# Triangle update: one stage for norm and fill, left and right through DRAM by eighths, products with strided operands

## The chip, the cores and the metric

The kernel runs on one core of a Trainium2 chip. The metric is the device time of one execution in microseconds (us), lower is better. The median of three runs before the change is 5121.33 us.

## The reference

An image of 256 x 256 positions with 128 channels (float32) passes through four layers, each of which normalises its input, applies an operation and adds the result to the input. The layers are a triangle attention, a gated recurrence, a triangle multiplication and a 3 x 3 convolution. The change touches only the third, whose core is:

```python
x = x + _L2_conv_ref(_gn(x), ...)          # layer 3 of 4; _gn normalises groups of 4 channels

pair_norm = layer_norm(pair, ln_in_w, ln_in_b)                       # over the 128 channels
p = jnp.einsum('bijd,hd->bijh', pair_norm, p_in_w)                   # 256 outputs: left 128, right 128
g = jax.nn.sigmoid(jnp.einsum('bijd,hd->bijh', pair_norm, g_in_w))
left = g[..., :H] * p[..., :H]
right = g[..., H:] * p[..., H:]
out = jnp.einsum('bikd,bjkd->bijd', left, right / jnp.float32(L))    # a 256 x 256 x 256 product per channel
out = layer_norm(out, ln_out_w, ln_out_b)
out = jnp.einsum('bijh,dh->bijd', out, p_out_w)
gate = jax.nn.sigmoid(jnp.einsum('bijd,ed->bije', pair_norm, g_out_w))
return gate * out
```

## The kernel before

Images lie in DRAM with the channel as the partition: `x2T` (the layer's input), `znT` (the normalised input), `prodD` (the products), `x3T` (the output), each 128 x 65,536 float32, 33.5 MB. The method `triangle` works on them in three stages, one after the other on the same core. Every operation in it is pinned, so each engine runs its operations in the order in which the program states them; `mm`, `act`, `tt`, `add` and `table` are such pinned forms of a matmul, a ScalarE activation, a VectorE product, a VectorE addition and a ScalarE table load. A float32 matmul in the source appears in the trace as two matmul instructions, each with its own weight load.

**Stage one (norm).** 32 loads of 2048 positions each. `load` brings `xin` from `x2T` on SyncE's queue. `centre` multiplies 1024 positions by a centring matrix (`zc`, a PSUM tile) and adds a bias (`zs`); `square` squares it on ScalarE; `variance` takes the mean over channels with four small matmuls (`var`) and forms `rs` = (var + eps)^-0.5 by `Ln` and `Exp`; `spreads` brings `rs` back to all partitions (`pr`). VectorE multiplies `zs` by `pr` to `zn`, GpSimd applies the affine part, and GpSimd's queue stores `zn` to `znT`. The activation tables of Ln and Exp and of the sigmoid are different ones, and each switch is a table load on ScalarE.

**Stage two (fill and products).** Four quarters of 32 channels. In each, all of `znT` is read again (`zt`, 64 blocks of 1024 positions); a chunk of 128 positions is the stationary operand and 128 columns of `wf` (32 channels for left and right, gate and value) are the moving one:

```python
for ch in range(8):
    o = (b % 2) * 1024 + ch * P
    mm(z[:, ch, :], zt[:, o:o + P], wf[:, g].rearrange("c t d -> c (t d)"))
```

ScalarE takes the sigmoid of the gates (`sg`), and VectorE writes value times gate into `LR`, which keeps a whole quarter in SBUF with the row index innermost, so that its elements are written 512 bytes apart. Then 32 products follow, one for each channel, each of four source matmuls with contiguous operands of `LR` into a PSUM tile `po`; ScalarE scales them into `o`, and GpSimd's queue stores `o` (256 KB) to `prodD`.

**Stage three** reads `znT`, `prodD` and `x2T` and makes `x3T`. Ahead of it `transformed_taps` prepares the convolution's weights. Neither is changed.

Of the kernel before, what the change touches and what calls it, by code (L numbers as in the profile page):

```python
# [9 lines left out]
F32 = mybir.dt.float32  # L10
# [7 lines left out]
P = 128  # L18
# [12 lines left out]
class Kernel:  # L31
# [24 lines left out]
    def table(self, name, key="table"):  # L56
        return self.chain(key, self.nc.scalar.preload_act_table_set(name))

    def mm(self, out, lhsT, rhs, start=True, stop=True):
        return self.nc.tensor.matmul(out, lhsT, rhs, start=start, stop=stop)  # L60
# [985 lines left out]
                        D[it - lag]["b"] = it - lag  # L1046
                        step(D[it - lag])

    def triangle(self, x2T, x3T, znT, prodD, stats2, shift2, stats3, prepare):

        nc, tc, I = self.nc, self.tc, self.i
        V = nc.vector
        NB, G, CQ = NPIX // 1024, 4, P // 4
        pin = lambda f: lambda *a, **k: tc.keep_in_program_order(f(*a, **k))  # L1056
        mm, act, copy = pin(self.mm), pin(self.act), pin(nc.scalar.copy)
        tt, ts, stt, bn = pin(V.tensor_tensor), pin(V.tensor_scalar), pin(V.scalar_tensor_tensor), pin(V.bn_stats)
# [3 lines left out]
        with ExitStack() as c:  # L1062
            wp = c.enter_context(self.pool(name="tw", bufs=1))
            with self.pool(name="twp", bufs=2, space=PSUM) as ps0:
                ab = self.group_affine(wp, ps0, stats2, self.g4, "2", shift=shift2)
                lc, cb = self.centering(wp, ps0, ab, "2")
                W = self.weights
                lnw, lnb, low, lob = (W[n] for n in ("in_w", "in_b", "out_w", "out_b"))
                wpg, oraw, we = W, W["o"], W["e"]
                pb = ps0.tile([P, 2], F32, name="tpbo", tag="gn")  # L1070
                self.mm(pb[:, 0:1], oraw, lob)
                wbo = wp.tile([P, 1], F32, name="twbo")
                V.tensor_copy(wbo, pb[:, 0:1])
                wo = wp.tile([P, P], F32, name="two")
                V.tensor_scalar_mul(wo, oraw, low)

                wf = wp.tile([P, G, 4, CQ], F32, name="wf")
                for n, m in enumerate("gp"):
                    for side in range(2):
                        V.tensor_copy(wf[:, :, 2 * n + side, :],  # L1080
                                      wpg[m][:, side * P:(side + 1) * P].rearrange("c (g d) -> c g d", g=G))

            quarters = c.enter_context(ExitStack())
            zp = quarters.enter_context(self.pool(name="tz", bufs=5))

# [7 lines left out]
            def variance(ps, work, sq):  # L1093

                var = ps.tile([P, 512], F32, name="var", tag="r", bufs=2)
                for k in range(4):
                    mm(var[32 * k:32 * k + 32], m32, sq[k // 2][:, (k % 2) * 512:(k % 2 + 1) * 512])
                rs = work.tile([P, 512], F32, name="rs")
                act(rs, var, AF.Ln, bias=self.eps)
                act(rs, rs, AF.Exp, scale=-0.5)  # L1100
                return rs

            def spreads(ps, rs):
                pr = [ps.tile([P, 1024], F32, name="pr", tag="w") for _ in range(2)]
                for k in range(4):
                    mm(pr[k // 2][:, (k % 2) * 512:(k % 2 + 1) * 512], spread[32 * k:32 * k + 32], rs[32 * k:32 * k + 32])
                return pr


            with ExitStack() as c1:  # L1110
# [3 lines left out]
                xin, sq, zs = {}, {}, {}  # L1114

                def load(m):
                    if m < NB // 2:
# [3 lines left out]
                def centre(m, b):  # L1121
                    if m >= NB // 2:
                        return
                    zc = ps.tile([P, 1024], F32, name="zc", tag="w")
                    for k in range(2):
                        s = b * 1024 + k * 512
                        mm(zc[:, k * 512:(k + 1) * 512], lc, xin[m][:, s:s + 512])
                    zs[m, b] = work.tile([P, 1024], F32, name="zs")
                    add(zs[m, b], zc, cb)

                def square(m, b):
                    if m < NB // 2:
# [3 lines left out]
                table(LN_EXP)  # L1136
                for m in range(2):
                    load(m)
                for b in range(2):
                    centre(0, b)  # L1140
                    square(0, b)
                for m in range(NB // 2):
                    load(m + 2)
                    centre(m + 1, 0)
                    rs = variance(ps, work, [sq[m, b] for b in range(2)])
                    square(m + 1, 0)
                    centre(m + 1, 1)
                    square(m + 1, 1)
                    pr = spreads(ps, rs)
                    zn = io.tile([P, 2048], F32, name="zn")  # L1150
                    for b in range(2):
                        z = zn[:, b * 1024:(b + 1) * 1024]
                        tt(z, zs[m, b], pr[b], MUL)
                        nc.gpsimd.tensor_scalar(z, z, lnw, lnb, MUL, ADD)
                    nc.gpsimd.dma_start(znT[:, m * 2048:(m + 1) * 2048], zn)

            with ExitStack() as c1:

                LR = c1.enter_context(self.pool(name="tl", bufs=1)).tile([P, 2, 2, 2 * CQ, P], F32, name="LR")
                work = c1.enter_context(self.pool(name="t2w", bufs=2))  # L1160
                io = c1.enter_context(self.pool(name="t2", bufs=3))
                ps = c1.enter_context(self.pool(name="t2s", bufs=2, space=PSUM))
                table(SIGMOID)
# [27 lines left out]
            quarters.close()  # L1191
            prepare(W["kt"], W["wd"], W["bv"])


# [270 lines left out]
    def run(self, ctx):  # L1465
# [12 lines left out]
        biasD = dram.tile([NH, NPIX], F32, name="biasD")  # L1478
        HD_ = dram.tile([2, 2 * KS, 4, N, HC // 4], F32, name="HD")
        prodD = image("prodD")  # L1480
        self.early = {n: [const.tile([P, 2], F32, name=f"early{k}{n}") for k in range(2)] for n in "3"}
        later = ctx.enter_context(self.pool(name="lw", bufs=1))
        with self.pool(name="aw", bufs=1) as wp:
# [10 lines left out]
        self.triangle(x2T, x3T, znT, prodD, stats["2"], shift2, stats["3"], lambda *a: self.transformed_taps(late(), *a))  # L1494
        self.convolution(x3T, stats["3"], late())


# [56 lines left out]
```

## Time and profile before

| | us |
|---|---|
| median of three runs | 5121.33 (5119.53 to 5126.31) |
| profiled execution, its own time | 5126.96 |
| profiled execution, span from the first to the last instruction | 5125.2 |
| mean granted TensorE clock | 0.988 of full speed |
| triangle, stage one: first `zc` to first `z` | 3243.6 to 3457.2 |
| triangle, stage two: first `z` to last `po` | 3457.2 to 4146.9 |
| triangle, stage three | from 4159.2 |

The durations come from the profiled execution, and its span is 1.8 us shorter than its own time. Times of the triangle are counted from the start of the span. In the profile, PE is TensorE's matmul, PEld its weight load, DVE is VectorE, ACT is ScalarE, POOL is GpSimd and SP is SyncE. A row of a group names the line, the engine, the operation, the written tile, the read tiles and their shapes, and how often it occurs, and then the busy time of the group (overlaps counted once), the mean duration of one in ns, and the time the engine stood idle ahead of it, with what ended that. L60 is the line of the helper through which every matmul goes, L54 that of every activation, L1056 that of the pinned operations of `triangle`, so these groups are told apart by their tiles.

### The profile page before, as it was taken

The page shows a single profiled execution, that of the slowest core. Times are in us where ns is not written, and L with a number is a line of the kernel's source. Part 1 is how long each engine was busy: PE and PEld are TensorE (multiplying, and loading weights), DVE is VectorE, ACT ScalarE, POOL GpSimd, SP SyncE. Part 2 cuts the span into 40 slices and gives each one's busy share as a digit, 9 for nine tenths or more (in the row PEclk, how much of TensorE's full clock was granted, in tenths as well). Part 3 has the DMA queues.
Part 4 walks back from the last instruction along what each step waited for, and adds up shares of the span by engine and source line. Part 5 has one row for each costly group of instructions (what it writes and reads, how often), then busy time and mean ns, then how long its engine had stood idle before and what let it go on. Part 6 is the DMA issues. An engine that isn't in the chain of part 4 may idle for free.

```text
span 5125.2 us, 78589 instructions
## 1 busy us (share of the span) xinstructions
PE 4948.5 (97%) x31357; PEld 2702.7 (53%) x31357; DVE 4100.7 (80%) x4797; ACT 3496.2 (68%) x4948; POOL 414.2 (8%) x600
## 2 busy tenths in 40 slices
PE   7999999999999899999999999899999989989999
PEld 2444555555555333333333333229999953349999
DVE  6666999999999799999999999675333537779886
ACT  5445888888888799999999999453333357762110
POOL 1332000000000000000000000240111010000000
PEclk9999999999999899999999999999999999999999
DMA  8794222222222122222222222687666678865432
GB/s 282 277 338 186 83 79 87 83 80 87 83 80 82 59 76 63 76 63 76 63 76 63 76 63 67 253 304 280 239 229 238 237 277 325 327 224 188 140 121 67
DMA packets 205054, 781.44 MB, mean 152 GB/s; under 512 B 56857, under 2 KB 60263, under 8 KB 155423
## 3 DMA queue, kind: packets, MB, share of 16 engines
q1 hardware_dynamic: 147070, 505.57, 29.3%
q0 software_dynamic: 56320, 270.42, 14.5%
q8 instruction: 250, 4.10, 0.3%
q14 instruction: 118, 0.96, 0.1%
q10 hardware_dynamic: 1296, 0.40, 0.0%
HBM read 504.94 MB, written 271.32 MB: 151 GB/s over the span
## 4 chain that ended last, share of the span: by engine, by line
PE 56%; DVE 28%; issue 5%; ACT 1%; DMA 1%; POOL 0%; POOLq 0%; DVEq 0%; SPq 0%; ACTq 0%
PE z L60 9%; PE m L60 7%; PE nd L60 7%; PE sc L60 5%; PE po L60 4%; PE zc L60 4%; DVE tr L896 3%; DVE t L893 3%; DVE y L893 3%; DVE p L893 3%; DVE yf L893 3%; PE ppq L60 3%; PE ppv L60 2%; PE px L60 2%; PE pe L60 2%
## 5 line engine op out<-in xcount | busy, mean ns | idle before, releaser
L559 DVE TENSOR_TENSOR e<-sc,bT 128x1024 f32<-128x1024 f32 x512 | 603.2, 1220 | 52.4 <-PE sc L60 51.2
L54 ACT ACTIVATE e<-e 128x1024 f32<-128x1024 f32 x512 | 540.5, 1056 | 63.0 <-DVE e L559 49.2
L1056 DVE TENSOR_TENSOR LR<-z,sg 128x512 f32<-128x512 f32 x256 | 268.2, 1049 | 365.0 <-ACT sg L54 365.0
L60 PE MATMUL m<-U,v 128*128 128x128 f32 x4608 | 517.6, 276 | 6.6 <-DVE v L1403 6.6
L60 PEld LDWEIGHTS m<-U,v 128*128 128x128 f32 x4608 | 517.4, 193 | 6.7 <-DVE v L1403 6.7
L60 PE MATMUL z<-wf,zt 128*128 128x128 f32 x4096 | 460.4, 276 | 2.1 <-DVE zn L1056 1.3
L60 PEld LDWEIGHTS z<-wf,zt 128*128 128x128 f32 x4096 | 460.0, 193 | 3.9 <-DVE zn L1056 2.8
L54 ACT ACTIVATE sg<-z 128x512 f32<-128x512 f32 x256 | 152.8, 597 | 309.9 <-PE z L60 308.0
L54 ACT ACTIVATE sq<-zs 128x1024 f32<-128x1024 f32 x192 | 202.4, 1054 | 196.4 <-DVE zs L370 156.8
L559 DVE TENSOR_TENSOR ks<-e 128x1024 f32<-128x1024 f32 x256 | 300.9, 1217 | 0.0
L60 PE MATMUL sc<-tq,tk 32*128 32x256 f32 x4096 | 298.2, 403 | 2.8 <-DVE e L559 1.9
L60 PE MATMUL nd<-e,tv 128*32 128x256 f32 x4096 | 272.0, 383 | 0.0
L60 PEld LDWEIGHTS sc<-tq,tk 32*128 32x128 f32 x4096 | 187.3, 185 | 160.5 <-issue 97.1
L54 ACT ACTIVATE dn<-dn 128x512 f32<-128x512 f32 x384 | 241.7, 629 | 13.3 <-DVE dn L559 2.6
L60 PE MATMUL av<-y,ident 128*128 128x512 f32 x384 | 191.3, 607 | 44.9 <-DVE y L893 44.9
L60 PE MATMUL po<-LR 128*128 128x256 f32 x1024 | 222.2, 380 | 6.9 <-DVE LR L1056 6.9
L1440 ACT COPY m4s<-m 128x512 f32<-128x512 f32 x32 | 18.7, 584 | 287.8 <-PE m L60 287.8
L60 PEld LDWEIGHTS po<-LR 128*128 128x128 f32 x1024 | 194.1, 190 | 34.2 <-DVE LR L1056 7.7
L60 PE MATMUL bx<-p,ident 128*128 128x512 f32 x384 | 193.3, 612 | 0.0
L54 ACT ACTIVATE o<-po 128x256 f32<-128x256 f32 x256 | 84.3, 381 | 145.4 <-issue 110.5
L60 PEld LDWEIGHTS nd<-e,tv 128*32 128x32 f32 x4096 | 120.3, 110 | 109.8 <-issue 44.2
L862 ACT ACT_TABLE_LOAD x132 | 169.4, 1283 | 1.6
(368 smaller groups left out, 10276.9 us busy)
## 6 DMA issues: line engine op xcount, KB each, us to landing
zt<-znT SPq DMA_DIRECT2D x128, 1024.0 KB
znT<-zn POOLq DMA_DIRECT2D x64, 1024.0 KB, 5.3
xin<-x2T SPq DMA_DIRECT2D x64, 1024.0 KB
xin<-in_x_dram SPq DMA_DIRECT2D x50, 1024.0 KB
xr<-x3T SPq DMA_DIRECT2D x46, 768.0 KB
xT<-xo POOLq DMA_DIRECT2D x32, 1024.0 KB, 9.2
xr<-xT SPq DMA_DIRECT2D x64, 512.0 KB
zn<-znT SPq DMA_DIRECT2D x64, 512.0 KB
```

The source lines that it names most:

```text
L54: return self.nc.scalar.activation(out, in_, func, bias=bias, scale=scale, **kw)
L60: return self.nc.tensor.matmul(out, lhsT, rhs, start=start, stop=stop)
L559: pin = lambda f: lambda *a, **k: tc.keep_in_program_order(f(*a, **k))
L862: pin(nc.scalar.preload_act_table_set(want))
L893: pin(V.tensor_tensor(out, a, b_, op))
L896: pin(V.scalar_tensor_tensor(out, a, k, b_, op0, op1))
L1056: pin = lambda f: lambda *a, **k: tc.keep_in_program_order(f(*a, **k))
L1440: nc.scalar.copy(m4, m[4])
```

## The change

The channels are now cut into eight eighths of 16 (`G, CQ = 8, P // 8`). Stage one and the fill become one stage: behind the norm of 2048 positions, all 256 channels of left and right are made at once from `zn` in SBUF, with 512 columns of `wf` as the moving operand. They go to a new DRAM image `LRD` of 8 x 128 x 16,384 float32, ordered by eighths. `znT` is still stored, but read only by stage three. The products then read one eighth at a time from `LRD` in four loads of 2 MB; the tile `LR` has two buffers of 64 KB per partition, and in it the channel lies innermost, so that both operands of a product matmul step over 128 elements (512 bytes) from one element to the next. The order of operations in the new stage is written out by hand, two loads at a time, with the table switched twice for each pair.

```diff
-        NB, G, CQ = NPIX // 1024, 4, P // 4
+        NB, G, CQ = NPIX // 1024, 8, P // 8
...
-                wf = wp.tile([P, G, 4, CQ], F32, name="wf")
+                wf = wp.tile([P, 2, G, 2, CQ], F32, name="wf")
...
+                            zs[m, b] = work.tile([P, 1024], F32, name="zs", bufs=8)
+                            add(zs[m, b], zc, cb)
+                        load(m + 2)
...
+                def scales(ms):
+                    var = {}
+                    for m in ms:
+                        var[m] = ps.tile([P, 512], F32, name="var", tag="r", bufs=2)
+                        for k in range(4):
+                            mm(var[m][32 * k:32 * k + 32], m32, sq[m, k // 2][:, (k % 2) * 512:(k % 2 + 1) * 512])
+                    table(LN_EXP)
+                    for m in ms:
+                        rs[m] = work.tile([P, 512], F32, name="rs")
+                        act(rs[m], var[m], AF.Ln, bias=self.eps)
+                        act(rs[m], rs[m], AF.Exp, scale=-0.5)
+                    table(SIGMOID)
+
+                def normalise(m):
+                    if m < NM:
+                        pr = spreads(ps, rs[m])
+                        zn[m] = work.tile([P, 2048], F32, name="zn")
+                        for b in range(2):
+                            z = zn[m][:, b * 1024:(b + 1) * 1024]
+                            tt(z, zs[m, b], pr[b], MUL)
+                            nc.gpsimd.tensor_scalar(z, z, lnw, lnb, MUL, ADD)
+                        nc.gpsimd.dma_start(znT[:, m * 2048:(m + 1) * 2048], zn[m])
+
+                def left_right(m, i):
+                    if not i:
+                        st[m] = work.tile([P, G, 4, 4, 2 * CQ], F32, name="st", bufs=2)
+                    z = ps.tile([P, 2, 512], F32, name="z", tag="w")
+                    for j in range(2):
+                        o = (2 * i + j) * P
+                        mm(z[:, j], zn[m][:, o:o + P], wf.rearrange("c n g s d -> c (n g s d)"))
+                    sg = work.tile([P, 2, 256], F32, name="sg")
+                    act(sg, z[:, :, :256], AF.Sigmoid)
+                    k = 2 * (i % 2)
+                    tt(st[m][:, :, i // 2, k:k + 2].rearrange("p g k f -> p k g f"),
+                       z[:, :, 256:].rearrange("p k (g f) -> p k g f", g=G), sg.rearrange("p k (g f) -> p k g f", g=G), MUL)
+                    if i == 7:
+                        nc.gpsimd.dma_start(LRD[:, :, m * 512:(m + 1) * 512].rearrange("g p n -> p g n"),
+                                            st[m].rearrange("p g x k f -> p g (x k f)"))
...
+                for m in range(0, NM, 2):
+                    for i in range(8):
+                        left_right(m, i)
+                    if m + 2 < NM:
+                        scales((m + 2, m + 3))
+                        centre(m + 4)
+                        centre(m + 5)
+                        normalise(m + 2)
+                    for i in range(8):
+                        left_right(m + 1, i)
+                        if i == 1:
+                            normalise(m + 3)
+                        if i % 2:
+                            square(m + 4 + i // 4, i // 2 % 2)
...
-                for g in range(G):
-
-                    for b in range(NB):
-                        if b % 2 == 0:
-                            zt = zp.tile([P, 2048], F32, name="zt")
-                            nc.sync.dma_start(zt, znT[:, b * 1024:(b + 2) * 1024])
-                        z = ps.tile([P, 8, P], F32, name="z", bufs=3)
-                        for ch in range(8):
-                            o = (b % 2) * 1024 + ch * P
-                            mm(z[:, ch, :], zt[:, o:o + P], wf[:, g].rearrange("c t d -> c (t d)"))
-                        sg = work.tile([P, 8, 2 * CQ], F32, name="sg")
-                        act(sg, z[:, :, :2 * CQ], AF.Sigmoid)
-                        rows = lambda t: t.rearrange("p (x q) f -> p x q f", x=2)
-                        tt(LR[:, :, :, :, 2 * b:2 * b + 2].rearrange("p a k f x -> p x (a k) f"),
-                           rows(z[:, :, 2 * CQ:]), rows(sg), MUL)
...
+                lp = c1.enter_context(self.pool(name="tl", bufs=2))
                 io = c1.enter_context(self.pool(name="t2", bufs=3))
-                ps = c1.enter_context(self.pool(name="t2s", bufs=2, space=PSUM))
+                ps = c1.enter_context(self.pool(name="t2s", bufs=4, space=PSUM))
                 for g in range(G):
+                    LR = lp.tile([P, P, 4, 2 * CQ], F32, name="LR")
+                    flat_lr = LR.rearrange("p x k f -> p (x k f)")
+                    for n in range(4):
+                        cols = slice(n * 4096, (n + 1) * 4096)
+                        nc.sync.dma_start(flat_lr[:, cols], LRD[g, :, cols])
                     for d in range(CQ):
                         po = ps.tile([P, 2, 2, P], F32, name="po")
                         for a in range(2):
                             for kc in range(2):
-                                mm(po[:, a], LR[:, a, kc, d, :], LR[:, :, kc, CQ + d, :], start=kc == 0, stop=kc == 1)
+                                mm(po[:, a], LR[:, :, 2 * a + kc, d],
+                                   LR[:, :, kc::2, CQ + d].rearrange("p x b -> p b x"), start=kc == 0, stop=kc == 1)
```

More of the change, by code (lines that the diff above doesn't have):

```diff
@@ L1047, in recurrence, with triangle @@
                         step(D[it - lag])
-    def triangle(self, x2T, x3T, znT, prodD, stats2, shift2, stats3, prepare):
+    def triangle(self, x2T, x3T, znT, prodD, LRD, stats2, shift2, stats3, prepare):
         nc, tc, I = self.nc, self.tc, self.i
         V = nc.vector
-        NB, G, CQ = NPIX // 1024, 4, P // 4
+        NB, G, CQ = NPIX // 1024, 8, P // 8
         pin = lambda f: lambda *a, **k: tc.keep_in_program_order(f(*a, **k))
@@ L1075, in triangle @@
                 V.tensor_scalar_mul(wo, oraw, low)
-                wf = wp.tile([P, G, 4, CQ], F32, name="wf")
+                wf = wp.tile([P, 2, G, 2, CQ], F32, name="wf")
                 for n, m in enumerate("gp"):
                     for side in range(2):
-                        V.tensor_copy(wf[:, :, 2 * n + side, :],
+                        V.tensor_copy(wf[:, n, :, side, :],
                                       wpg[m][:, side * P:(side + 1) * P].rearrange("c (g d) -> c g d", g=G))
-            quarters = c.enter_context(ExitStack())
-            zp = quarters.enter_context(self.pool(name="tz", bufs=5))
             m32 = wp.tile([P, 32], F32, name="tmean")
@@ L1107, in spreads @@
                 return pr
+            NM = NB // 2
             with ExitStack() as c1:
@@ L1113, in triangle, with centre @@
                 ps = c1.enter_context(self.pool(name="t1s", bufs=3, space=PSUM))
-                xin, sq, zs = {}, {}, {}
+                xin, sq, zs, rs, zn, st = {}, {}, {}, {}, {}, {}
                 def load(m):
-                    if m < NB // 2:
+                    if m < NM:
                         xin[m] = io.tile([P, 2048], F32, name="xin")
                         nc.sync.dma_start(xin[m], x2T[:, m * 2048:(m + 1) * 2048])
[L1121 to L1129, printed above, removed]
+                def centre(m):
+                    if m < NM:
+                        for b in range(2):
+                            zc = ps.tile([P, 1024], F32, name="zc", tag="w")
+                            for k in range(2):
+                                s = b * 1024 + k * 512
+                                mm(zc[:, k * 512:(k + 1) * 512], lc, xin[m][:, s:s + 512])
+                            zs[m, b] = work.tile([P, 1024], F32, name="zs", bufs=8)
+                            add(zs[m, b], zc, cb)
+                        load(m + 2)
@@ L1131, in square @@
                 def square(m, b):
-                    if m < NB // 2:
+                    if m < NM:
                         sq[m, b] = work.tile([P, 1024], F32, name="sq")
                         act(sq[m, b], zs[m, b], AF.Square)
-                table(LN_EXP)
+                def scales(ms):
[10 more added lines that the diff above has]
+                    table(SIGMOID)
@@ new lines, in normalise @@
+                def normalise(m):
+                    if m < NM:
+                        pr = spreads(ps, rs[m])
+                        zn[m] = work.tile([P, 2048], F32, name="zn")
+                        for b in range(2):
+                            z = zn[m][:, b * 1024:(b + 1) * 1024]
+                            tt(z, zs[m, b], pr[b], MUL)
+                            nc.gpsimd.tensor_scalar(z, z, lnw, lnb, MUL, ADD)
+                        nc.gpsimd.dma_start(znT[:, m * 2048:(m + 1) * 2048], zn[m])
@@ L1137, in triangle @@
                 for m in range(2):
                     load(m)
[L1139 to L1150, printed above, removed]
-                    for b in range(2):
[L1152 to L1155, printed above, removed]
+                for m in range(2):
+                    centre(m)
+                    for b in range(2):
+                        square(m, b)
@@ new lines, in triangle @@
+                scales((0, 1))
+                for m in range(2, 4):
+                    centre(m)
+                for m in range(2):
+                    normalise(m)
+                for m in range(2, 4):
+                    for b in range(2):
+                        square(m, b)
+                for m in range(0, NM, 2):
[12 more added lines that the diff above has]
+                            square(m + 4 + i // 4, i // 2 % 2)
@@ L1157, in triangle @@
             with ExitStack() as c1:
-                LR = c1.enter_context(self.pool(name="tl", bufs=1)).tile([P, 2, 2, 2 * CQ, P], F32, name="LR")
-                work = c1.enter_context(self.pool(name="t2w", bufs=2))
+                lp = c1.enter_context(self.pool(name="tl", bufs=2))
                 io = c1.enter_context(self.pool(name="t2", bufs=3))
-                ps = c1.enter_context(self.pool(name="t2s", bufs=2, space=PSUM))
-                table(SIGMOID)
+                ps = c1.enter_context(self.pool(name="t2s", bufs=4, space=PSUM))
@@ L1189, in triangle @@
                                             o.rearrange("p a j b -> p a (j b)"))
-            quarters.close()
             prepare(W["kt"], W["wd"], W["bv"])
@@ L1480, in run @@
         prodD = image("prodD")
+        LRD = dram.tile([8, P, NPIX // 4], F32, name="LRD")
         self.early = {n: [const.tile([P, 2], F32, name=f"early{k}{n}") for k in range(2)] for n in "3"}
@@ L1492, in late @@
             return pools[0]
-        self.triangle(x2T, x3T, znT, prodD, stats["2"], shift2, stats["3"], lambda *a: self.transformed_taps(late(), *a))
+        self.triangle(x2T, x3T, znT, prodD, LRD, stats["2"], shift2, stats["3"], lambda *a: self.transformed_taps(late(), *a))
         self.convolution(x3T, stats["3"], late())
```

## The prediction

> **What bounds the kernel now.** I read the page's busy shares first, then the chain of waits, then the busy time by stretches of the stages that the diff touches, then the groups with their shapes.
>
> ```profile
> PE 4948.5 (97%) x31357; PEld 2702.7 (53%) x31357; DVE 4100.7 (80%) x4797; ACT 3496.2 (68%) x4948; POOL 414.2 (8%) x600
> ```
>
> TensorE is busy almost throughout, so a change must take TensorE time away or fill its gaps. The chain (start us, length us, engine, tile, line, count) shows what the triangle's second stage is made of:
>
> ```profile
> 3632.04 114.36 PE z L60 x1024
> 3748.12 55.67 PE po L60 x256
> ...
> 4204.82 3.43 PE py L60 x8
> ```
>
> One quarter is 1024 fill matmuls in 114.36 us (111.7 ns each, 128 columns) and 256 product matmuls in 55.67 us (217 ns, 256 columns). The third row gives 512 columns: 3.43/8 = 429 ns. All three are 0.84 to 0.87 ns a column: TensorE itself is the limit. (Each float32 matmul of the source is two instructions; counts are instructions.)
>
> Stretches (us, busy of each engine, granted clock, DMA share, GB/s):
>
> ```profile
> 3300.00:3440.00 140.00, 130.00 (x520) 39.62 (x524) 103.18 (x88) 71.20 (x86) 62.67 (x64) 0.99 0.91 342
> 3305.00:3310.00 5.00, 5.00 (x21) 1.40 (x20) 1.80 (x2) 2.26 (x3) 0.57 (x1) 0.73 1.02 433
> 3465.00:3578.00 113.00, 110.73 (x983) 110.39 (x984) 66.28 (x64) 37.01 (x62) 0.00 (x0) 1.00 0.83 294
> 3578.00:3632.00 54.00, 54.00 (x253) 47.54 (x252) 0.00 (x0) 20.40 (x62) 16.73 (x31) 1.00 0.40 153
> ```
>
> The first stage (first row) repeats every 6.33 us and moves 342 GB/s, near what DMA gives; its TensorE columns need far less than its busy time suggests: 8 centring matmuls (3.43 us) and two bursts of 8 small ones (var 1.06, pr 1.14 us in the timeline, of which 0.16 each is drain) make 5.3 us. The second row is the highest DMA rate, 433 GB/s; from 3270 to 3315 us it is 391 to 433, and I use 415. Fill and products (last rows) are pure TensorE. The tile's first and last times give the whole: first zc at 3243.6, first z at 3457.2, last product at 4146.9 us: **903.3 us**, of which 213.6 before the fill.
>
> The groups that price the new operands (engine, operation, tiles, shapes, count | busy us, mean ns | idle before):
>
> ```profile
> L60 PE MATMUL po<-LR 128*128 128x256 f32 x1024 | 222.2, 380 | 6.9 <-DVE LR L1056 6.9
> L1056 DVE TENSOR_TENSOR LR<-z,sg 128x512 f32<-128x512 f32 x256 | 268.2, 1049 | 365.0 <-ACT sg L54 365.0
> L893 DVE TENSOR_TENSOR d<-pa,ff 128x512 f32<-128x512 f32 x64 | 43.2, 675 | 4.4 <-PE pa L60 4.4
> L181 ACT COPY H<-ph 128x512 f32<-128x512 f32 x16 | 16.5, 1032 | 20.5 <-PE ph L60 20.5
> L1440 ACT COPY m4s<-m 128x512 f32<-128x512 f32 x32 | 18.7, 584 | 287.8 <-PE m L60 287.8
> ```
>
> Rows two and four write 512 elements to SBUF with steps of 512 and 64 bytes, rows three and five write them contiguously: 1049 against 675 ns, 1032 against 584. A step costs 0.73 and 0.87 ns more an element.
>
> [...] No engine reads SBUF with such a step in the kernel before, so for reads nothing is shown. [...] in the 433 GB/s stretch both queues ran.
>
> **The change part by part.**
> 1. *Merged first stage, TensorE.* Fill: 512 chunks x 2 instructions x 429 ns = 439 us (before 4 x 116 = 464). Centring: 256 x 429 = 110. Variance and spreads: 32 x (0.90 + 0.98) = 60. Together 609 us. Gaps: the head (centre, square, table, Ln, Exp, table, spread, scale before the first z) leaves TensorE some 7 us idle; per pair of loads the z tile waits about 1.2 us for one of three PSUM buffers, which two spreads hold while VectorE drains them (2 x 1.21 us) behind four centring adds (1.28 each): 16 x 1.2 = 19. **635 us against 678 before (213.6 + 464): -43.** Bounds: no gaps, -69; twice the gaps, -17.
> 2. *Behind it, at no cost* as long as a load takes 19.8 us on TensorE: ScalarE, a load: two squares 2.11, Ln and Exp 1.32, eight sigmoids 4.78, half of two table loads 1.28, total 9.5. VectorE: 2 x 1.28 + 2 x 1.21 + 8 x 0.68 (the store is now contiguous; at most 1.05) = 10.4 to 13.4. POOL: two scalings 2.37, two DMA issues (0.57 each on this page; the strided one perhaps 1.2). DMA: 1 MiB in and 3 MiB out, 212 GB/s of 415. The 32 table loads added stand behind the last sigmoids on ScalarE; TensorE has four centring tiles (6.9 us) to do meanwhile, against 5.2 us of tables, Ln and Exp.
> 3. *SP and POOL queues.* 128 zt loads (1 MiB) go; 32 LRD stores (2 MiB, POOL) and 32 LR loads (2 MiB, SP) come: the same 134 MB. An LR load waits in SP's queue for its stores; behind it stand only further LR loads and, after them, the third stage's loads, which wait for the last product anyhow.
> 4. *Handover.* The built order lets the first eighth's first three loads start before the stage ends, as they wait only for loads 0 to 23. The fourth waits for the last store: 2.1 MB at 415 = 5 us plus some 2.8 (a 1 MiB store here lands in 5.3 us, 2.5 of it transfer), and then the same to read. **+15 us**, 10 to 20.
> 5. *Products, DMA.* An eighth: 8.4 MB in, 4.2 MB out, 30.3 us at 415, against 16 x 8 x 217 ns = 27.7 us of TensorE at the old pace. If that pace held, DMA would set it: 27.7 + 6 x 30.3 + 27.7 = 237 us, +15.
> 6. *Products, TensorE.* Moving and stationary operands now step 512 bytes from element to element. Not shown before; nearest rows: the two strided writes. Lower bound: nothing, 217 ns. Upper: +0.87 ns a column, 441 ns. A gain is excluded, as the column rate is already TensorE's own. I take **a doubling, 434 ns**: a float32 column takes 0.84 ns[...]. Weights (128 elements) would take some 215 ns and hide under 434. Then 1024 x 434 = 444 us, an eighth takes 55.6 us and hides its 30.3 us of DMA: **+222 over the old pace**.
>
> Sum: 635 + 15 + 444 = 1094 us against 903.3: +191. Against the profiled execution (span 5125.2, time 5126.96) that is a span near 5316; the median of the runs, 5121.33, is 5.6 lower than the profiled time, so **5312 us**.
>
> **The rivals.**
> *A. Strided reads cost TensorE nothing* (faster). [...] Then DMA sets the products: 635 + 15 + 237 = 887, -16, 5105 us; with DMA above 455 GB/s, 872, -31, 5090. It decides as long as a product matmul stays under (903.3 - 650)/1024 = 247 ns: 0.12 ns a column separates gain from loss.
> *B. Free reads, but DMA at 342 GB/s as in the first stage*, because 2 KB stores mix with the loads (o has three buffers; a late store stops ScalarE, then TensorE). An eighth takes 36.9 us, 277 in all: 927, +24, 5145 us. Against it: 433 GB/s with both queues running.
> *C. The change doesn't do what it says* (loads not ahead, stage one still a chain of waits): the built order shows spreads and squares interleaved with the fill, so only the gaps of part 1 are open.
>
> **How the numbers follow.** Doubling 0.54, A 0.36, B 0.10. The likeliest case's own range: 404 to 441 ns a matmul (414 to 452 us) and +-15 for the rest, 5266 to 5335. The range takes in A: 5090 to 5330. About 0.2% (10 us) is what a measurement of this kernel can tell from no change. Faster: most of A, 0.32. Same: A with slow gaps, 0.08. Slower: 0.60.
>
> **What would show it.** Right: po<-LR near 434 ns apart, an eighth about 55 us, DMA under half busy there, fill matmuls 429 ns, last fill some 635 us after the first zc. Wrong: po at 217 ns with waits on LR loads (A or B, told apart by the GB/s); a first stage much over 650 us; the first product more than 20 us after the last fill.

## The result, and the profile after

The change makes the kernel **slower: 5319.31 us** (median of four runs, 5315.3 to 5320.15) against 5122.89 us of the kernel before on the same chip, a ratio of 1.0382 with a 95% interval of 1.0364 to 1.0400. The forecast was 5312 us.

In the profiled execution of after (its own time 5320.15 us, span 5318.4) the triangle runs from the first `zc` at 3238.4 to the last product at 4338.5 us: 1100.1 us against 903.3, that is +196.8. The two spans differ by 193.2, so what lies outside the triangle takes 3.6 us less and explains none of the loss. Engine, busy us (share of the span), instructions:

```profile
PE 5141.0 (97%) x28285; PEld 2545.9 (48%) x28285; DVE 4011.6 (75%) x4797; ACT 3529.6 (66%) x4978; POOL 444.0 (8%) x632
```

TensorE has 3072 instructions fewer and is busy 192 us longer: its instructions have become slower, not its waits longer. The chain of waits (start us, length us, what) has the end of the first stage and the whole of the products:

```profile
3804.41 3.69 PE z L60 x8
...
3809.49 24.32 PE z L60 x56
...
3843.32 38.12 PE z L60 x88
...
3882.80 15.06 issue
3897.86 440.66 PE po L60 x1024
...
4350.63 5.30 PE pe L60 x8
```

In the first stage the chain follows the fill in stretches. The 1.4 us between two of them (3804.41 + 3.69 to 3809.49) are not idle: TensorE does the eight matmuls of the next spread there (1.14 us) and stands still for 0.34. Then there is the handover of 15.06 us ("issue" is a time in which the profile shows no releaser; here the first eighth has just been stored and is being read back), and after it 1024 product matmuls without a gap: 440.66/1024 = 430 ns each, where it was 217. The stretches (us, PE, PEld, DVE, ACT and POOL busy, granted clock, DMA share, GB/s) show which resource is left idle; the first row is the whole first stage, the second a part of it, the third the products:

```profile
3238.40:3881.40 643.00, 629.58 (x1792) 257.38 (x1792) 330.67 (x383) 294.87 (x415) 122.79 (x127) 1.00 0.56 212
3300.00:3440.00 140.00, 137.78 (x397) 56.53 (x396) 69.85 (x84) 66.54 (x96) 25.02 (x26) 1.00 0.52 195
3898.00:4338.00 440.00, 440.00 (x1024) 300.06 (x1025) 0.00 (x0) 83.64 (x254) 68.67 (x127) 0.99 0.52 208
```

The first stage, which DMA and a chain of waits had held before, is now TensorE's, 98% busy with DMA at about half its rate. So are the products. The groups with their shapes (busy us, mean ns | idle before, what ended it):

```profile
L60 PE MATMUL po<-LR 128*128 128x256 f32 x1024 | 440.7, 607 | 16.4 <-issue 16.4
L60 PEld LDWEIGHTS po<-LR 128*128 128x128 f32 x1024 | 300.1, 293 | 157.0 <-issue 17.2
L1056 DVE TENSOR_TENSOR st<-z,sg 128x512 f32<-128x512 f32 x256 | 176.9, 691 | 245.5 <-ACT sg L54 242.5 <-DMA LRD<-st 2.9
```

The mean duration of a pipelined matmul (607 ns, before 380) is longer than its pace; the pace is busy time by count. The weight load has grown too, 293 ns where before it took 190, so two strided operands could each be the cause. The contiguous store on VectorE takes 691 ns in place of 1049.

### The profile page after: what moved, and what is told of

It is laid out like the page before. It is cut to its first block, busy times and chain, and to the rows that moved or that the text cites. A ratio compares the mean times of both kernels' runs of the same rounds, so it can differ in the third digit from the quotient of the medians.

```text
span 5318.4 us, 72309 instructions
## 1 busy us (share of the span) xinstructions
PE 5141.0 (97%) x28285; PEld 2545.9 (48%) x28285; DVE 4011.6 (75%) x4797; ACT 3529.6 (66%) x4978; POOL 444.0 (8%) x632
## 3 DMA queue, kind: packets, MB, share of 16 engines
q0 software_dynamic: 73216, 337.53, 17.2%
## 4 chain that ended last, share of the span: by engine, by line
PE 58%; DVE 27%; issue 5%; ACT 1%; POOL 0%; DMA 0%; POOLq 0%; DVEq 0%; ACTq 0%; SPq 0%
PE z L60 8%; PE po L60 8%; PE m L60 7%; PE nd L60 7%; PE sc L60 5%; PE zc L60 4%; DVE tr L896 3%; DVE t L893 3%; DVE y L893 3%; DVE p L893 3%; DVE yf L893 3%; PE ppq L60 3%; PE ppv L60 2%; PE px L60 2%; PE pe L60 2%
## 5 line engine op out<-in xcount | busy, mean ns | idle before, releaser
L60 PE MATMUL z<-wf,zn 128*128 128x512 f32 x1024 | 447.4, 595 | 10.9 <-DVE zs L1056 5.6
L60 PE MATMUL po<-LR 128*128 128x256 f32 x1024 | 440.7, 607 | 16.4 <-issue 16.4
L60 PEld LDWEIGHTS po<-LR 128*128 128x128 f32 x1024 | 300.1, 293 | 157.0 <-issue 17.2
L1056 DVE TENSOR_TENSOR st<-z,sg 128x512 f32<-128x512 f32 x256 | 176.9, 691 | 245.5 <-ACT sg L54 242.5
L60 PEld LDWEIGHTS z<-wf,zn 128*128 128x128 f32 x1024 | 191.9, 190 | 266.3 <-issue 246.9
```

## The experiments

Four questions were open: which of the two strided operands costs the time; by what rule; whether the transfers of the new layout have a part in it; and whether the rest of the change would gain if the stride cost nothing, as rival A had it, or lose, as rival B had it. Of the kernels below, four take the operands of their products from other places of the same tile, and so compute other products, with the same instruction counts and sizes; they are named where they come up. Kernels with one run only are compared by the durations in their profiles.

### Which operand: one of the two made contiguous

`weights_plain` keeps the moving operand strided and reads the stationary one contiguously, from another place in `LR`:

```diff
-                                mm(po[:, a], LR[:, :, 2 * a + kc, d],
+                                mm(po[:, a], flat_lr[:, (2 * a + kc) * 4096 + d * P:(2 * a + kc) * 4096 + (d + 1) * P],
```

> The changed kernel with the stationary operand of the products read contiguously from the wrong place in LR (its products are therefore of other elements); the moving operand keeps its 512-byte step. Theory M (the moving operand's strided read sets the pace): po stays at 430 ns a matmul and the time at 5319 us within 10, while the weight load falls from 293 to 190 ns. Theory W (the weight load sets the pace): po falls to 217 ns or to DMA's pace, the time to about 5110 us.

`moving_plain` does the opposite, and `both_plain` both:

```diff
-                                   LR[:, :, kc::2, CQ + d].rearrange("p x b -> p b x"), start=kc == 0, stop=kc == 1)
+                                   flat_lr[:, (2 * a + kc) * 4096 + 1920 + d * P:(2 * a + kc) * 4096 + 1920 + (d + 2) * P].rearrange("p (b x) -> p b x", b=2), start=kc == 0, stop=kc == 1)
```

> The changed kernel with the moving operand of the products read contiguously from the wrong place in LR; the stationary operand keeps its 512-byte step. Theory M: po falls to 217 to 230 ns a matmul, weight loads still 293 ns and hidden; products then take DMA's pace, about 237 us, time about 5115 us. Theory W: po stays near 430 ns, time 5319 us.

> The changed kernel with both operands of the products read contiguously from the wrong places in LR: what the rest of the change is worth. Rival A's sum for the products: DMA at 415 GB/s gives 237 us and a time of about 5105 to 5120 us; if TensorE still set it, 222 us and some 5100 us; rival B (342 GB/s): 277 us and 5150 us.

Measured: 5318.13 us with plain weights, 5169.44 with a plain moving operand (one run each), and 5166.7 with both (four runs; ratio to before 1.0081, 1.0064 to 1.0098). The groups of `weights_plain`:

```profile
L60 PE MATMUL po<-LR 128*128 128x256 f32 x1024 | 442.4, 609 | 16.7 <-issue 16.7
L60 PEld LDWEIGHTS po<-LR 128*128 128x128 f32 x1024 | 212.3, 207 | 246.8 <-issue 245.7
```

The weight loads are down to 207 ns (190 in the kernel before) and the products still take 442 us. The two rows of `moving_plain`, with ScalarE's eviction:

```profile
L60 PE MATMUL po<-LR 128*128 128x256 f32 x1024 | 243.1, 396 | 60.2 <-ACT o L54 43.7 <-issue 16.4
L60 PEld LDWEIGHTS po<-LR 128*128 128x128 f32 x1024 | 230.7, 304 | 73.1 <-ACT o L54 54.2 <-issue 17.2
L54 ACT ACTIVATE o<-po 128x256 f32<-128x256 f32 x256 | 84.0, 381 | 219.5 <-DMA prodD<-o 145.6 <-PE po L60 46.0 <-issue 26.5
```

Here the weight loads are the slow ones (304 ns) and TensorE is busy for 243 us. **The moving operand alone sets the pace; the stationary operand's slower load is hidden** (TensorE is busy for 442.4 us with contiguous weights, for 440.7 in after). But what was expected of the rest was missed: the products of `moving_plain` were to take 237 us and took 287 (3900.7 to 4187.5), and `both_plain` was to take 5105 to 5120 us, or 5150 under rival B, and took 5166.7. The new wait stands in the first and the last row: TensorE waits 43.7 us for ScalarE, and ScalarE 145.6 us for stores of `o`.

### Not the transfers: the stride put into the kernel before

`before_strided` is the kernel before, without any transfer in its products, with `LR` laid out the other way round. Both operands then step over 256 elements, and VectorE writes contiguously:

```diff
-                LR = c1.enter_context(self.pool(name="tl", bufs=1)).tile([P, 2, 2, 2 * CQ, P], F32, name="LR")
+                LR = c1.enter_context(self.pool(name="tl", bufs=1)).tile([P, P, 2, 2, 2 * CQ], F32, name="LR")
...
-                        tt(LR[:, :, :, :, 2 * b:2 * b + 2].rearrange("p a k f x -> p x (a k) f"),
+                        tt(LR[:, 2 * b:2 * b + 2].rearrange("p x a k f -> p x (a k) f"),
...
-                                mm(po[:, a], LR[:, a, kc, d, :], LR[:, :, kc, CQ + d, :], start=kc == 0, stop=kc == 1)
+                                mm(po[:, a], LR[:, :, a, kc, d], LR[:, :, :, kc, CQ + d].rearrange("p x a -> p a x"), start=kc == 0, stop=kc == 1)
```

> The kernel before with one part of the change alone: LR has the channel innermost, so VectorE stores contiguously (about 690 ns in place of 1049) and both product operands are strided (256 elements). If the strided moving operand alone makes the slowdown: po 430 ns a matmul, products 440 us in place of 222, fill unchanged because TensorE sets it, time 5123 + 218 = about 5341 us. If the two parts interact (the strided read is dear only beside the LR loads), about 5123 us.

Measured: 5341.84 us (one run; before on that chip 5127.13). Its chain, where before it had 55.67 us for 256 products:

```profile
3572.47 110.44 PE po L60 x256
3682.91 114.36 PE z L60 x1024
```

110.44/256 = 431 ns at a step of 1024 bytes, against 430 at 512 bytes: whether the step is 512 or 1024 bytes makes no difference, nor do the loads and stores beside the products. Four quarters lose 4 x (110.4 - 55.7) = 219 us; the contiguous store (692 ns in place of 1049) gives nothing back, as VectorE had time to spare (365.0 us idle ahead of these stores in the kernel before, 619.1 here).

### The rule: a sweep of the step

`step_sweep` gives each eighth a step of its own for the moving operand, with contiguous weights and ten buffers for `o`; its operands are thus not those of the product:

```diff
-                io = c1.enter_context(self.pool(name="t2", bufs=3))
+                io = c1.enter_context(self.pool(name="t2", bufs=10))
...
+                                step, o0 = (1, 2, 3, 4, 8, 12, 1, 2)[g], (2 * a + kc) * 4096 + d * 32
+                                mm(po[:, a].rearrange("p b x -> p (b x)"), flat_lr[:, o0:o0 + P],
+                                   flat_lr[:, o0:o0 + 256 * step:step], start=kc == 0, stop=kc == 1)
```

> The changed kernel with ten o buffers and with product operands read from the wrong places in LR: the stationary one contiguous, the moving one with a step of 1, 2, 3, 4, 8, 12, 1, 2 elements in the eight eighths. Only the spacing of the product matmuls in each eighth is read. [...]steps 1 and 2 give 217 ns, step 3 lies between, steps 4, 8 and 12 give 430 ns alike. Step theory (any step above one halves the rate): 430 ns from step 2 on. Distance theory (far steps cost more than near ones): 4, 8 and 12 differ, and lie under the 430 ns of the 128-element step.

The whole took 5210.08 us (one run). In each eighth the product matmuls start at an even distance, and that distance is the pace. These are their rows in six stretches, for steps of 1, 2, 3, 4, 8 and 12 elements (count, durations in ns, first and last start in us):

```profile
L60 PE MATMUL po<-LR x118: 379/379/379, 4173.7 to 4199.0; 128*128 128x256 f32 x118
L60 PE MATMUL po<-LR x112: 386/388/388, 3927.8 to 3952.9; 128*128 128x256 f32 x112
L60 PE MATMUL po<-LR x111: 508/510/510, 3957.5 to 3994.9; 128*128 128x256 f32 x111
L60 PE MATMUL po<-LR x108: 629/631/634, 4004.5 to 4052.9; 128*128 128x256 f32 x108
L60 PE MATMUL po<-LR x105: 639/639/641, 4059.7 to 4107.6; 128*128 128x256 f32 x105
L60 PE MATMUL po<-LR x109: 623/624/640, 4114.5 to 4162.8; 128*128 128x256 f32 x109
```

The time from the first to the last start, by the number of intervals:

| step (elements) | bytes | ns a matmul of 256 columns |
|---|---|---|
| 1 | 4 | 25.3/117 = 216 |
| 2 | 8 | 25.1/111 = 226 |
| 3 | 12 | 37.4/110 = 340 |
| 4 | 16 | 48.4/107 = 452 |
| 8 | 32 | 47.9/104 = 461 |
| 12 | 48 | 48.3/108 = 447 |
| 128 (`after`) | 512 | 430 |
| 128, contiguous weights (`weights_plain`) | 512 | 432 |
| 256 (`before_strided`) | 1024 | 431 |

The penalty does not grow with the distance once the step is 16 bytes: 452 ns there, 430 at 512 and 431 at 1024 bytes. It is small at 8 bytes (226 against 216) and complete at 16. From 8 to 16 bytes the time goes with the step: 226 ns at 8 bytes is half of the 452 at 16, and at 12 bytes three quarters of it would be 339 ns, against 340 measured. At 4 bytes it does not fall further with the step: 216 ns, the contiguous pace. The first of the three expectations fits, but for 226 ns in place of 217 at a step of 2 and for the long steps: 4, 8 and 12 are not quite alike, and all three cost 4 to 7% more than the 430 to 432 ns of the long steps, where the expectation had one value for all. Why the doubling is complete at 16 bytes, and what makes this small difference, the runs do not show.

### The rest of the change without the stride

`moving_runs4` takes the product's operands without the long step in the moving one. The right half of the staged tile is laid out so that four row indices of one channel follow each other, 16 bytes, and the moving operand reads in runs of four. The left half stays strided as the stationary operand. VectorE writes the two halves separately:

```diff
-                    tt(st[m][:, :, i // 2, k:k + 2].rearrange("p g k f -> p k g f"),
-                       z[:, :, 256:].rearrange("p k (g f) -> p k g f", g=G), sg.rearrange("p k (g f) -> p k g f", g=G), MUL)
+                    zv, gv = (t.rearrange("p k (g s d) -> p s k g d", g=G, s=2) for t in (z[:, :, 256:], sg))
+                    left = st[m][:, :, i // 2, :P // 2].rearrange("p g (k d) -> p k g d", k=4)[:, k:k + 2]
+                    right = st[m][:, :, k:k + 2, P // 2:].rearrange("p g k (d x) -> p k g d x", x=4)[:, :, :, :, i // 2]
+                    tt(left, zv[:, 0], gv[:, 0], MUL)
+                    tt(right, zv[:, 1], gv[:, 1], MUL)
...
-                    LR = lp.tile([P, P, 4, 2 * CQ], F32, name="LR")
+                    LR = lp.tile([P, P // 4, 4, P], F32, name="LR")
+                    LL = LR.rearrange("p x y f -> p (x y) f")
...
-                                mm(po[:, a], LR[:, :, 2 * a + kc, d],
-                                   LR[:, :, kc::2, CQ + d].rearrange("p x b -> p b x"), start=kc == 0, stop=kc == 1)
+                                mm(po[:, a].rearrange("p b (x y) -> p b x y", y=4), LL[:, :, (2 * a + kc) * CQ + d],
+                                   LR[:, :, kc::2, P // 2 + 4 * d:P // 2 + 4 * d + 4].rearrange("p x b y -> p b x y"),
+                                   start=kc == 0, stop=kc == 1)
```

> The changed kernel with the right half laid out so that four row indices lie side by side (16 bytes), the moving operand then reads runs of four elements[...]; the stationary operand keeps its 512-byte step. VectorE stores left and right with two instructions, the right one with a 16-byte step, some 1.0 us in place of 0.69 per chunk pair, hidden behind 1.72 us of TensorE. Theory M[...]: 217 to 230 ns a matmul, time as moving_plain, 5105 to 5125 us. If it is the step or the break in the pattern as such that costs[...]: 300 to 430 ns, 5190 to 5319 us.

Measured: 5167.34 us (four runs), ratio to before 1.0083 (1.0066 to 1.0100). So, with three buffers for `o`, the stride costs 152 us of the 196, and **what is left of the change still loses 0.8%**. The expected 5105 to 5125 us was missed, although the matmul itself keeps the expected pace where nothing holds it up (in the last eighth 125 of them start between 4159.7 and 4186.8 us, 219 ns apart). The products run from 3904.5 to about 4187.7 us, 283 us, close to the 287 of `moving_plain`. The groups show where TensorE and ScalarE wait, and the timeline how (start us, length us, engine, count [idle before, what ended it]):

```profile
L60 PE MATMUL po<-LR 128*128 128x256 f32 x1024 | 241.8, 394 | 58.4 <-ACT o L54 41.5 <-issue 16.9
L54 ACT ACTIVATE o<-po 128x256 f32<-128x256 f32 x256 | 83.2, 382 | 217.0 <-DMA prodD<-o 155.8 <-PE po L60 41.1 <-issue 19.9
```

```profile
3987.96 0.66 ACT L54 ACTIVATE o<-po 128x256 f32<-128x256 f32 x2 [2.98 <-DMA prodD<-o]
3988.67 2.11 PE L60 MATMUL po<-LR 128*128 128x256 f32 x8 [1.42 <-ACT o L54]
...
3991.07 0.66 ACT L54 ACTIVATE o<-po 128x256 f32<-128x256 f32 x2 [2.45 <-DMA prodD<-o]
3991.78 2.10 PE L60 MATMUL po<-LR 128*128 128x256 f32 x8 [1.01 <-ACT o L54]
```

ScalarE waits for a store of `o` to land so that one of the three buffers comes free, and then TensorE waits for ScalarE, which frees the PSUM tile. Each pair of evictions here releases just one product (8 matmul instructions): the stores' landing has become the pace. That is the wait that rival B named. The test is to give `o` more buffers.

`runs4_o10` is `moving_runs4` with ten:

```diff
-                io = c1.enter_context(self.pool(name="t2", bufs=3))
+                io = c1.enter_context(self.pool(name="t2", bufs=10))
```

> The runs-of-four kernel with ten o buffers in place of three. Theory S (stores of prodD queue behind LR loads, three buffers cannot bridge it, ScalarE and then TensorE stop): the waits of o on prodD stores vanish, the products shrink from 285 to between 225 and 250 us, TensorE's or DMA's pace, and the time falls from 5167 to about 5125 us. Theory D (DMA simply has no more than 343 GB/s for this mixture): products stay at 280 to 290 us and the time at 5165 us, the waits move to LR loads.

Measured: 5125.9 us (13 runs), ratio to before 0.9998 (0.9990 to 1.0006). Its groups:

```profile
L60 PE MATMUL po<-LR 128*128 128x256 f32 x1024 | 232.1, 389 | 25.2 <-issue 17.2 <-ACT o L54 6.5 <-DMA LR<-LRD 1.4
L54 ACT ACTIVATE o<-po 128x256 f32<-128x256 f32 x256 | 84.0, 381 | 173.4 <-issue 72.9 <-DMA prodD<-o 57.2 <-PE po L60 42.2
```

TensorE's idle time ahead of products falls from 58.4 us to 25.2, of which 17.2 is the handover. The products take 240 us (3905.7 to 4145.9), 43 less. The expectation that ScalarE's waits for the stores vanish was met in part: they fall from 155.8 us to 57.2, and TensorE is held up by them for only 6.5.

The stores of `o` in `moving_runs4` in the DMA issues (count, KB, median us from issue to landing), first from 3975 to 4000 us, while the four loads of the next eighth run, then from 4002 to 4013 us, when these have ended:

```profile
prodD<-o POOLq DMA_DIRECT2D x8, 256.0 KB, 9.0
```

```profile
prodD<-o POOLq DMA_DIRECT2D x9, 256.0 KB, 2.5
```

And over the stretch from 3940 to 4140 us, first `moving_runs4`, then `runs4_o10`:

```profile
prodD<-o POOLq DMA_DIRECT2D x85, 256.0 KB, 4.8
```

```profile
prodD<-o POOLq DMA_DIRECT2D x108, 256.0 KB, 12.4
```

With ten buffers the single store takes longer, 12.4 us, and yet 108 in place of 85 fit into the same 200 us. The transfers' rate over this stretch, in 40 slices of 5 us, says why; again first `moving_runs4`, then `runs4_o10`:

```profile
GB/s 338 426 413 441 402 190 207 314 396 446 401 435 220 207 214 377 428 423 434 383 158 225 358 419 422 448 403 239 142 284 409 433 430 424 256 170 240 390 426 442
```

```profile
GB/s 388 419 450 418 381 403 423 431 424 441 391 410 432 431 423 416 393 291 404 437 412 434 406 424 416 422 420 438 401 405 372 405 428 429 414 411 288 161 157 157
```

With three buffers the rate swings with a period of about seven slices, the time of an eighth of the products: while the next eighth's 8.4 MB come in, it is mostly above 400, and the stores beside the loads land late and stop TensorE (the timeline's rows lie in slices of 446 and 401); once they are in, only stores are left, and DMA falls to half its rate (190 and 207 GB/s in the first two such slices). Its mean is 345 GB/s. The view of 3975 to 4000 us has 1.57 MB of stores in 25 us, six products, where TensorE at 8 x 217 ns a product would make fourteen. As an estimate from these numbers, some eight finished products must wait for their store in every eighth: three buffers cannot hold them, ten can. So ten buffers let TensorE work through the first phase, and its stores fill the second: the mean is 390, and 412 over the first 36 slices, after which the loads have ended. Products and DMA now look like this, the first seven eighths and then the last one, beside which there are no loads (us, PE, PEld and ACT busy on the products, granted clock, DMA share, GB/s):

```profile
3905.70:4117.20 211.50, 203.54 (x896) 199.32 (x896) 72.77 (x222) 0.99 0.99 405
4117.20:4145.90 28.70, 28.51 (x128) 28.24 (x128) 10.61 (x33) 1.00 0.52 201
```

An eighth takes 30.2 us (211.5/7) with DMA 99% busy, and 28.7 with TensorE the limit. DMA is the bound, as rival A had it, if only by 1.5 us an eighth, and the kernel is as fast as before, not faster.

### The two gaps

What is left idle on TensorE in `runs4_o10` are the handover (17.2 us) and the start of stage three (from 4145.9 to 4158.4 us, 12.5 us, where the convolution's weights are made ready and the first loads arrive; in the kernel before it is the same). `runs4_o10_early` makes the weights ready at the start of the products and cuts the first eighth's last load so that little of it waits for the last store:

```diff
+                prepare(W["kt"], W["wd"], W["bv"])
                 for g in range(G):
...
-                    for n in range(4):
-                        cols = slice(n * 4096, (n + 1) * 4096)
-                        nc.sync.dma_start(flat_lr[:, cols], LRD[g, :, cols])
+                    cuts = [0, 4096, 8192, 12288] + [15872] * (g == 0) + [16384]
+                    for c_0, c_1 in zip(cuts, cuts[1:]):
+                        nc.sync.dma_start(flat_lr[:, c_0:c_1], LRD[g, :, c_0:c_1])
...
-            prepare(W["kt"], W["wd"], W["bv"])
```

> As runs4_o10, and with two more edits: the convolution's weights are prepared at the start of the product stage instead of behind it, and the last LR load of the first eighth is cut so that only 512 columns wait for the last store. The 15 us between fill and products then hold the preparation and shrink to about 10, and the 12 us between the last product and the third stage's first matmul shrink to a few us: about 15 us less than runs4_o10, near 5110 us, a little faster than before.

Measured: **5111.86 us** (seven runs), ratio to before 0.9973 (0.9962 to 0.9984): 0.3% faster than the kernel before, and faster than after. The last product and the first matmul of stage three, in the rows of their tiles:

```profile
L60 PE MATMUL po<-LR x1024: 379/380/776, 3897.7 to 4141.3; 128*128 128x256 f32 x171
```

```profile
L60 PE MATMUL pe<-zn,w2e x256: 592/592/697, 4142.5 to 4562.1; 128*128 128x512 f32 x128
```

The gap ahead of stage three is under 1 us; the handover went from 17 to 12 us (the last fill matmul starts at 3884.8 us, the first product at 3897.7). The products themselves take 4 us longer, with the preparation among them. Together that makes some 13 us, against a measured difference of 14.0 between the two medians. How much each of the two edits gives was not tried apart.

## Why the prediction was right, and where it was not

**Right: where the loss lies, and the doubling.** Step 6 took 434 ns a product matmul, by analogy with ScalarE's and VectorE's strided writes; 430 was measured, 440.7 us in place of 444 for the whole. That the weights' slower load hides was right as well; it is 293 ns, more than the 215 of the step. The sum was +191 us for the triangle; it became +197. The result of 5319 us lies in the range of 5090 to 5330, but that range is wide: it held a gain of 0.6% as well.

**The size was in part luck.** The factor of two was the author's estimate: the rows of the two strided writes, from which it was taken, say 1032/584 = 1.77 for ScalarE and 1049/675 = 1.55 for VectorE. Added as time for each element, the same rows gave 404 to 441 ns, and no row of TensorE bore on it; the step said so. What holds for TensorE came from the sweep: some 1.7 to 1.8 ns a column at steps of 16 bytes and more (430/256 to 461/256), twice the 0.84 ns of a contiguous one.

**Part by part.**

| step of the prediction | predicted | measured |
|---|---|---|
| 1: merged first stage (first `zc` to last `z`) | 635 us (609 to 661) | 3238.4 to 3881.4: 643 |
| 2: VectorE's store; POOL's issue of a 2 MiB store | 0.68 us; perhaps 1.2 | 0.69; 0.91 |
| 4: handover, TensorE's idle time | 15 us, 10 to 20 | 16.4 |
| 5: DMA's pace in the products, if they are free | 415 GB/s, 237 us | 412 GB/s, 240 us, but only with ten buffers |
| 6: products | 444 us | 440.7 |

Step 1 has the largest error of these, 8 us, and it is the rest of two larger ones. TensorE is busy for 629.6 us in this stage where the step had 609: the groups of after have 447.4 us for the fill (439 in the step) and 117.2 for the centring (110), so the row of 429 ns an instruction, taken from a tight sequence of eight, was short for 437 and 458. The gaps, on the other hand, are 13 us (643.0 - 629.6) and not 26. That DMA is half idle and the first stage becomes TensorE's was right (212 GB/s over the stage, as estimated).

**Wrong: the price of rival A and the weight of rival B.** Rival A stood for free reads, and gave 237 us for the products and 5105 us in all; most of the 0.32 for faster lay there. With the stride's cost taken away and little else, the kernel takes 5167 us. The step of A's sum that failed is number 5: it set TensorE's 27.7 us for an eighth against DMA's 30.3 and took the larger one, as if both could run without a break. The buffers between them were left out: three of 256 KB for `o`, which with stores that land in 9 us beside the loads (2.3 us in the kernel before) do not last. B named the wait in its brackets, and came out at 277 us, where 283 to 287 were measured. That its rate fits too (342 GB/s; 345 measured between 3940 and 4140 us of `moving_runs4`) is chance: B took the rate from another stage and laid it to stores of 2 KB pieces mixed with loads, while here DMA does mostly over 400 as long as both run, and the mean is pulled down by the phases without loads. B got a chance of 0.10 because of one row, the 433 GB/s with both queues running. That row is a stretch of 5 us in another stage, with stores of 1 MiB; it says nothing on a loop that is closed through three small buffers. With ten, A's 237 us become right (240). (The chances do not quite add up either: 0.32 for faster and 0.08 for the same make 0.40, more than A's 0.36, from which both were to come.) Its gain of 16 us still doesn't come: the first stage of `runs4_o10` takes 647 us, not 635 (4 more than in after: VectorE stores each chunk pair with two instructions, and TensorE's waits for that store grow from 5.1 us to 8.8), the handover 17, not 15, and 647 + 17 + 240 = 904 us, the 903.3 of before.

So the forecast's number was carried by its one unknown, taken by analogy, and the split of the rest was too kind to the change: with contiguous moving operands, too, it was slower by 0.8%.

**Open.** Whether runs of two elements would do as well as those of four in the full kernel was not tried; the sweep's step of 2 suggests it. Nor was the number of buffers between three and ten, nor whether smaller loads of `LR`, or loads spread over the eighth, would let the stores land sooner. What makes steps of 16 to 48 bytes slightly dearer than those of 512 stays open.

## What to carry to other kernels

Before an operand is turned to make its producer's writes contiguous, look at the step with which the *moving* operand is then read: here a float32 matmul of 256 columns kept its pace within 5% at a step of 8 bytes (226 ns against 216) and in runs of four elements (219 ns), and took about twice as long at steps of 16 bytes and more (430 to 461 ns). The stationary operand could be strided at little cost (128 columns, beside matmuls of 256: TensorE busy for 243.1 us, with contiguous weights 235.8). Where bulk loads are put beside a loop with small stores, count the buffers behind the stores by the landing time that they will have then (here 9.0 us), not by the one that they have now (2.3 us). And where a stage only trades TensorE's time for DMA's, look at the gaps at its two ends: here the trade broke even (904 us against 903), and the gain of 0.3% came with the two gaps.

## What the runs showed of the hardware that was not expected

- The penalty for the moving operand is complete at a step of 16 bytes, and a longer distance hardly changes it: 430 to 461 ns for steps from 16 to 1024 bytes, 340 at 12 bytes, 226 at 8 and 216 at 4.
- A strided weight load of 128 columns takes 293 ns in after, in place of 190 in the kernel before, 1.5 times and not twice. It hides almost wholly even beside matmuls at the contiguous pace: in `moving_plain` TensorE is busy for 243.1 us, in `both_plain`, where the weights are contiguous too, for 235.8.
- Stores of 256 KB that land in 2.3 us in the kernel before take 9.0 us beside loads of 2 MiB when three are allowed, and 12.4, as the median of 200 us with and without loads, when ten are; the longer queue gave the higher rate (390 against 345 GB/s).
